# A gather that waits for the landing of the gather two ahead of it, in a graph layer on one Trainium2 core

## The chip, the cores and the metric

The kernel runs on one core of a Trainium2 chip. A core has a matrix engine (TensorE, PE in the profile; its weight loads are a row of their own, PEld), a vector engine (VectorE, DVE), an engine for pointwise functions (ScalarE, ACT), GpSimd (POOL) and a queue engine (SyncE, SP). Each engine runs its own instructions in the order in which they were built and waits on semaphores for the others. Transfers run on 16 DMA engines; a transfer raises a semaphore when its data has landed. The metric is the device time in microseconds (us) of one execution.

## The reference

Every node has a row of 128 floats. The rows are normalised, each node sums the normalised rows of its neighbours, and a small network works on the mean:

```python
N, E, D, H = 12500, 200000, 128, 512      # the sizes that come in
h = jnp.maximum(_layernorm(x, axis=-1), 0.0)
msgs = h[src]                                              # 200,000 rows, in any order
agg = jax.ops.segment_sum(msgs, dst, num_segments=n)       # dst is sorted
deg = jax.ops.segment_sum(ones, dst, num_segments=n)
agg = agg / jnp.maximum(deg, 1.0)[:, None]
t = jax.nn.relu(agg @ Wg + h @ Ws + bg)
t = jnp.tanh(t @ W1 + b1)
t = jnp.tanh(t @ W2 + b2)
return x + (t @ W3 + b3)
```

The edges are sorted by `dst`, so edges that stand together end at nodes that stand together. `src` is random: row by row, `h[src]` reads from anywhere in the table.

## The kernel before

**Setup.** The rows of `x` are normalised in pieces and stored to a table `htab` in DRAM (lines 210 to 228). The source indices are turned so that column `c` of `scol` holds the 128 indices of chunk `c` (lines 180 to 202). There are 1563 chunks of 128 edges. For 80 of them ("raw" chunks) the rows of `x` itself are gathered at the very start (line 132), and normalised later on DVE; for the other 1483 the rows come out of `htab` once it is written.

**A gather.** `gather(c)` (line 290) takes a tile `rows` of 128 x 128 floats (64 KB) from a ring of `AHEAD` = 40 buffers and issues one indirect DMA on GpSimd's queue: partition p receives the table's row that `scol[p, c]` names. GpSimd itself makes the descriptors of the transfer; that is the `DMA_INDIRECT` instruction of the profile. The engine does nothing else between the 80 raw gathers and the end.

**What a gather waits for.** Two waits stand in the built program. The first comes from the tile framework: GpSimd's transfers use eight landing semaphores in turn, so the sequencer holds a gather back, with an event instruction of its own, until the transfer that used the same semaphore last has landed, which is the gather eight ahead. The second wait stands in the gather itself: PE must have read the rows that lay in its buffer before, those of the gather 40 ahead.

**The use.** `add(c)` (line 412) multiplies the rows of a chunk by a one-hot matrix `oh` that DVE has made (`onehot`, line 339): the sum by node comes out of PE. Each of these products is two matmul records in the profile, `agg<-oh,rows` or `edge<-oh,rows`. The network's layers for blocks of 512 nodes (`layers`, line 589, and the parts that it strings together) are mixed between the products of the chunks. A loop over the chunks (line 635) writes the whole order down: it calls `gather` so far ahead that 40 chunks are open (line 651), then `add(c)`, then a step of a block's layers. PE, ACT and the stores on SP keep that order (`keep_in_program_order`). From chunk `QUICK` = 1312 on, the order of the layers' steps is planned with a pace of 1.251 us a gather (line 658), and the last blocks are small, so that little is left after the last chunk.

Of the kernel before, what the change touches and what calls it, by code (L numbers as in the profile page):

```python
# [34 lines left out]
BLK = 512  # L35
PIECE = 14
GRP = 8
NRAW = 10
RAW0 = 256
STEP = 40  # L40
# [15 lines left out]
def windowed(ctx, tc, x, src, dst, Wg, Ws, bg, W1, b1, W2, b2, W3, b3, out, flag):  # L56
    nc = tc.nc
# [12 lines left out]
    NCOL = NROW * CPR  # L70
    RAW1 = RAW0 + NRAW * STEP
    per = N * P // E
    assert D == P and H % P == 0 and per * E == N * P and RAW0 % GRP == STEP % GRP == 0
    assert all(c % GRP == 0 for c, _ in WINDOWS) and RAW1 <= WINDOWS[1][0]


    def raw(c):
        return RAW0 <= c < RAW1 and (c - RAW0) % STEP < GRP

# [3 lines left out]
    def first(w, span=per):  # L83
        return (span - w) // 2

    def window(c):
        if raw(c):
            return per * (c - c % GRP) + first(W_RAW, per * GRP), W_RAW
        w = [w for c0, w in WINDOWS if c0 <= c][-1]
# [20 lines left out]

    rsrc = const.tile([P, NRAW, GRP], I32, name="rsrc")
    rdst = const.tile([P, NRAW, GRP], I32, name="rdst")
    for t, a in ((rsrc, src), (rdst, dst)):
        a = a[RAW0 * P : RAW1 * P].rearrange("(u e) -> u e", u=NRAW)[:, : GRP * P]

        for u0, u1 in ((0, 1), (1, NRAW)):
            nc.sync.dma_start(t[:, u0:u1], a[u0:u1].rearrange("u (p k) -> p u k", p=P))
# [10 lines left out]
    raw_rows = []  # L128
    for g in range(NRAW):
        t = raws.tile([P, GRP, D], F32, name=f"raw{g}")  # L130
# [139 lines left out]

    ed = ctx.enter_context(tc.tile_pool(name="ed", bufs=3))
    ml = ctx.enter_context(tc.tile_pool(name="ml", bufs=2))
    rows_t, ohs, acc = {}, {}, {}

    class pe:

# [12 lines left out]

    def gather(c):  # L290
        r = rows_in.tile([P, D], F32, name="rows")
        nc.gpsimd.indirect_dma_start(  # L292
            out=r, out_offset=None, in_=htab,
            in_offset=bass.IndirectOffsetOnAxis(ap=scol[:, c : c + 1], axis=0),
        )
        rows_t[c] = r


# [336 lines left out]
    for c in range(NCH):  # L635
# [15 lines left out]
        while nxt < len(order) and nxt < behind + AHEAD:  # L651
            gather(order[nxt])
            nxt += 1
# [367 lines left out]
@with_exitstack  # L1021
def gnn_kernel(ctx: ExitStack, tc: tile.TileContext, *args):
    nc = tc.nc
    keep = ctx.enter_context(tc.tile_pool(name="flags", bufs=1))
    flag = keep.tile([1, 1], I32, name="flag")
    with ExitStack() as inner:
        windowed(inner, tc, *args, flag)
    outside = nc.values_load(flag, min_val=0, max_val=P)
    with tc.If(outside > 0):
        with ExitStack() as inner:  # L1030
            general(inner, tc, *args)
# [31 lines left out]
```

## Time and profile before

| | |
|---|---|
| median of 3 runs | 2302.71 us (2298.98 to 2318.72) |
| the profiled execution's own time | 2288.5 us |
| its span, first to last instruction | 2286.0 us |
| first and last gather out of `htab` start at | 119.9 us and 2237.4 us |
| first and last product of gathered rows start at | 123.6 us and 2271.9 us |
| mean granted clock of PE | 0.784 |
| data moved by GpSimd's queue | 102.53 MB in 50016 packets, 17.2% of 16 engines' time |

The page gives busy time by engine, a picture of the span in 40 slices, the DMA queues, the chain of work that ended last, and groups of like instructions. For a stretch of time, the trace lists each instruction with its start, its length and, in brackets, how long the engine stood idle before it and what ended that. "issue" there is time in which the engine waited for nothing that the profile shows, and "remote" a release whose source it can't name. Waits of a sequencer (the front of an engine, which reads instructions and waits on their semaphores) have records too, marked with a q (POOLq).

### The profile page before, as it was taken

What the parts mean: (1) busy time and instruction counts of PE and PEld (TensorE: products, weight loads), DVE (VectorE), ACT (ScalarE), POOL (GpSimd) and SP (SyncE); (2) the same over time, 40 slices, a digit from 0 to 9 for tenths busy, and PEclk for the clock granted to TensorE, in tenths of its full rate; (3) what the DMA queues carried; (4) which work ended last, traced back from release to release, by engine and by line L of the source; (5) the groups of instructions that cost most, each with busy time, mean ns of one, the idle gap of its engine ahead of it and who ended that gap; (6) DMA issues with size and microseconds to landing.
All of it is one profiled execution on the core that took longest, in us unless ns stands there. A gap on an engine that the chain in (4) does not pass through costs nothing.

```text
span 2286.0 us, 15134 instructions
## 1 busy us (share of the span) xinstructions
PE 1300.2 (57%) x4838; PEld 817.6 (36%) x4838; DVE 865.2 (38%) x1534; ACT 216.3 (9%) x352; POOL 1547.1 (68%) x1571
## 2 busy tenths in 40 slices
PE   0052263664687657666436655657646467576747
PEld 0031241342454434344224332334323234243536
DVE  5851390252353524244133331333523233233422
ACT  1100000000110101011001000101100001011112
POOL 7666676676676667677766666766676676766760
PEclk9999675786787879777777767778777778687879
DMA  6622111212221222122122121221221212122210
GB/s 171 189 80 54 46 50 47 56 46 61 57 60 48 59 59 60 46 61 58 52 57 60 45 59 48 60 60 47 58 66 42 61 48 74 48 62 56 57 51 16
DMA packets 120031, 139.03 MB, mean 61 GB/s; under 512 B 30742, under 2 KB 94098, under 8 KB 119748
## 3 DMA queue, kind: packets, MB, share of 16 engines
q0 software_dynamic: 50016, 102.53, 17.2%
q1 hardware_dynamic: 66766, 32.13, 5.2%
q10 hardware_dynamic: 3160, 3.31, 0.5%
q8 instruction: 40, 0.66, 0.1%
q14 instruction: 49, 0.40, 0.1%
HBM read 125.05 MB, written 12.82 MB: 60 GB/s over the span
## 4 chain that ended last, share of the span: by engine, by line
PE 44%; issue 26%; another core or an unknown queue 15%; DVE 5%; POOL 5%; DMA 2%; ACT 1%; SPq 0%; POOLq 0%; DVEq 0%; ACTq 0%
PE pm L279 25%; PE agg L279 14%; POOL rows L292 5%; PE edge L279 5%; DMA rows<-htab,scol 2%; ACT h L303 1%; PE pt L282 1%; DVE oh L347 1%; DVE h L176 1%; DVE agg L162 1%; DVE xt L163 1%; DMA xt<-in_x_dram 1%; DVE agg L169 1%; DVE fours L367 0%
## 5 line engine op out<-in xcount | busy, mean ns | idle before, releaser
L292 POOL DMA_INDIRECT rows<-htab,scol x1483 | 1469.0, 991 | 664.9 <-issue 300.1
L279 PE MATMUL pm<-h,w 128*128 128x512 f32 (+4 forms) x1344 | 708.0, 617 | 346.8 <-issue 189.5
L279 PE MATMUL agg<-oh,rows 128*128 128x144 f32 (+3 forms) x2122 | 447.4, 328 | 322.2 <-issue 241.5
L347 DVE TENSOR_TENSOR oh<-shared,dloc 128x1152 f32<-128x1152 f32 (+2 forms) x186 | 244.4, 1318 | 937.6 <-remote 392.2
L279 PEld LDWEIGHTS agg<-oh,rows 128*128 128x128 f32 x2122 | 387.4, 223 | 574.3 <-issue 470.3
L279 PEld LDWEIGHTS pm<-h,w 128*128 128x128 f32 x1344 | 234.2, 210 | 424.0 <-issue 251.4
L279 PE MATMUL edge<-oh,rows 128*128 128x144 f32 (+2 forms) x844 | 172.4, 316 | 87.3 <-issue 79.6
L279 PEld LDWEIGHTS edge<-oh,rows 128*128 128x128 f32 x844 | 149.2, 213 | 198.6 <-issue 179.0
L367 DVE TENSOR_TENSOR fours<-oh 128x704 bf16<-128x704 f32 x185 | 163.5, 884 | 2.3
L303 ACT ACTIVATE h<-pm,b2c 128x512 f32<-128x512 f32 (+4 forms) x112 | 70.8, 632 | 884.4 <-remote 429.1
L303 ACT ACTIVATE h<-pm,b1c 128x512 f32<-128x512 f32 (+4 forms) x112 | 69.2, 632 | 326.7 <-remote 163.1
L132 POOL DMA_INDIRECT raw<-in_x_dram,rsrc x80 | 77.2, 965 | 25.7 <-issue 24.1
L399 DVE RECIPROCAL rd<-rd 128x512 f32<-128x512 f32 (+4 forms) x28 | 81.8, 2920 | 0.0
L367 DVE TENSOR_TENSOR twos<-fours 128x384 bf16<-128x384 bf16 (+1 forms) x195 | 66.8, 343 | 2.4
L397 DVE TENSOR_SCALAR rd<-pm 128x512 f32<-128x512 f32 (+4 forms) x28 | 17.4, 621 | 127.1 <-remote 91.6
L461 DVE TENSOR_TENSOR mT<-agg,sums 128x136 f32<-128x136 f32 (+6 forms) x57 | 15.4, 271 | 120.7 <-remote 54.6
L194 PE MATMUL pm<-ident,idx_f 98*128 98x98 f32 x32 | 6.2, 377 | 89.1 <-DVE idx_f L190 56.0
L579 DVE TENSOR_TENSOR o<-pt,xb 128x512 f32<-128x512 f32 x23 | 15.8, 689 | 106.1 <-remote 50.9
L380 DVE TENSOR_TENSOR deg<-deg,cnt 128x200 bf16<-128x200 bf16 (+5 forms) x279 | 54.3, 221 | 2.6
L279 PE MATMUL agg<-ohr,raw 128*128 128x160 f32 x112 | 32.5, 387 | 35.0 <-issue 35.0
L367 DVE TENSOR_TENSOR cnt<-twos 128x200 bf16<-128x200 bf16 (+1 forms) x195 | 48.2, 247 | 3.2
L306 ACT COPY hT<-pt 128x512 f32<-128x512 f32 (+1 forms) x25 | 14.4, 577 | 350.2 <-remote 170.0
(75 smaller groups left out, 509.5 us busy)
## 6 DMA issues: line engine op xcount, KB each, us to landing
rows<-htab,scol POOLq DMA_INDIRECT x1483
hb<-htab SPq DMA_DIRECT2D x24, 256.0 KB
xb<-in_x_dram SPq DMA_DIRECT2D x23, 256.0 KB
out_dram<-o SPq DMA_DIRECT2D x23, 256.0 KB
htab<-h SPq DMA_DIRECT2D x6, 896.0 KB
xt<-in_x_dram SPq DMA_DIRECT2D x5, 896.0 KB
raw<-in_x_dram,rsrc POOLq DMA_INDIRECT x80
w<-in_L_gnn_W_dram ACTq DMA_DIRECT2D x1, 1024.0 KB
```

What stands on the lines that cost most here:

```text
L132: nc.gpsimd.indirect_dma_start(out=t[:, j, :], out_offset=None, in_=x, in_offset=bass.IndirectOffsetOnAxis(ap=rsrc[:, g, j : j + 1], axis=0),)
L162: nc.vector.tensor_reduce(stats[:, 0], xt, AX.X, ALU.add)
L163: nc.vector.scalar_tensor_tensor(xt, spread(stats[:, 0], k), -1.0 / D, xt, op0=ALU.mult, op1=ALU.add)
L169: nc.vector.tensor_reduce(stats[:, 1], sq, AX.X, ALU.add)
L176: nc.vector.scalar_tensor_tensor(h, xt, 0.0, spread(stats[:, 1], k), op0=ALU.max, op1=ALU.mult)
L279: tc.keep_in_program_order(nc.tensor.matmul(*a, **k))
L292: nc.gpsimd.indirect_dma_start(out=r, out_offset=None, in_=htab, in_offset=bass.IndirectOffsetOnAxis(ap=scol[:, c : c + 1], axis=0),)
L303: tc.keep_in_program_order(nc.scalar.activation(*a, **k))
L347: nc.vector.tensor_tensor(oh[:, :k, :w], lane[:, None, :w].to_broadcast([P, k, w]), dloc[:, g * GRP : g * GRP + k][:, :, None].to_broadcas ...
L367: nc.vector.tensor_tensor(out[:, :half, :full], ins[:, :half, :full], shifted(ins, half, half, lead, full), op=ALU.add)
L380: nc.vector.tensor_tensor(d, d, cnt[:, a0 - lo : a1 - lo], op=ALU.add)
L399: nc.vector.reciprocal(rd[:, :m], rd[:, :m])
```

## The change

Each gather but the first two is given a dependence on the landing of the gather that stands two ahead of it. `landing` is a list of the gathers' names in the order of issue.

```diff
+BEHIND = 2
...
-    rows_t, ohs, acc = {}, {}, {}
+    rows_t, ohs, acc, landing = {}, {}, {}, []
...
     def gather(c):
         r = rows_in.tile([P, D], F32, name="rows")
-        nc.gpsimd.indirect_dma_start(
+        dma = nc.gpsimd.indirect_dma_start(
             out=r, out_offset=None, in_=htab,
             in_offset=bass.IndirectOffsetOnAxis(ap=scol[:, c : c + 1], axis=0),
         )
+        if len(landing) >= BEHIND:
+            tc.add_manual_dep(
+                dma.ins, landing[-BEHIND], mybir.DependencyInfo(mybir.DependencyClass.Sync, mybir.DependencyReason.DATA),
+                reason="a gather begins when the one two before it has landed",
+            )
+        landing.append(dma.ins.name)
         rows_t[c] = r
```

In the built program a gather still has one event instruction and its own wait on PE. The event instruction now names the semaphore of the gather two ahead; that the gather eight ahead has landed follows from it. The ring of 40 buffers, the eight semaphores, the order on every engine and the data are the same, and GpSimd's program has two event instructions more.

## The prediction

> **What bounds the kernel now.** I start with the page's busy times:
>
> ```profile
> PE 1300.2 (57%) x4838; PEld 817.6 (36%) x4838; DVE 865.2 (38%) x1534; ACT 216.3 (9%) x352; POOL 1547.1 (68%) x1571
> ```
>
> No engine is full. POOL is the busiest, and nearly all of that is gathers, so I ask next what a gather waits for (the trace's answer on line 292):
>
> ```profile
> L292 POOL DMA_INDIRECT rows<-htab,scol x1483: 938/944/2728, 119.9 to 2237.4; - x186
> L292 POOLq EVENT_SEMAPHORE  x1450: 17/17/21711, 97.3 to 2235.2; - x182
> its engine sat idle before it (us, times) until:
>   issue: 300.1, 962
>   remote: 115.3, 76
>   PE agg L279: 102.4, 152
>   DMA rows<-htab,scol: 46.9, 154
>   PE pm L279: 43.7, 77
>   PE edge L279: 35.5, 54
> ```
>
> The reader is to see that 962 of the gathers start after 300.1 us of plain "issue", 0.31 us each, and that the landing of another gather (the DMA row) cost 46.9 us in 154 cases, also 0.30 each: no gather lost anything to the landing eight ahead. What did cost time is PE, through the ring of buffers. Unhindered, a gather comes every 0.944 + 0.30 = 1.245 us (the rows below). From 119.9 to 2237.4 the 1482 steps took 1.429 us each, so 272 us went to long gathers and to waits for PE. In the trace the time from a gather's start to the first use of its rows has a median of 38.7 us; only 84 of the 1483 rows are used within 3.4 us. So now **PE paces the ring** at 1.43 us a chunk, and gathers are some 30 chunks early. The limit that stands next is GpSimd at 1.245 us.
>
> **The change part by part.** It removes the wait for eight back, which costs nothing. It adds a wait that makes a loop: gather n-2 starts, lands, the sequencer sees it, gather n starts. Two such loops run side by side, so the new pace is half of one loop, or 1.245 us, or PE's 1.43 us, whichever is longest. The loop has two terms.
>
> *Start to landing.* A stretch in which PE waits for rows shows it from above:
>
> ```profile
> 172.10 0.94 POOL L292 DMA_INDIRECT rows<-htab,scol  x1 [0.30 <-DMA rows<-htab,scol]
> 173.35 0.95 POOL L292 DMA_INDIRECT rows<-htab,scol  x1 [0.30 <-issue]
> ...
> 174.75 0.82 PE L279 MATMUL agg<-oh,rows 128*128 128x144 f32 x2 [0.53 <-DMA rows<-htab,scol]
> ...
> 175.83 0.61 PE L279 MATMUL agg<-oh,rows 128*128 128x144 f32 x1 [0.27 <-DMA rows<-htab,scol]
> ```
>
> The gather of 172.10 is used at 174.75 and that of 173.35 at 175.83: 2.65 and 2.48 us. Over all rows that PE waited for, the least is 2.47, the usual 2.5 to 2.65, and about one in eight is near 3.2. From below, the gather before a gap in the queue, with the bytes moved (40 slices of the stretch from 812 to 822 us, 0.25 us each, in GB/s):
>
> ```profile
> 812.69 0.94 POOL L292 DMA_INDIRECT rows<-htab,scol  x1 [0.30 <-issue]
> 818.33 1.00 POOL L292 DMA_INDIRECT rows<-htab,scol  x1 [4.70 <-PE pm L279]
> ```
>
> ```profile
> GB/s 82 0 0 0 229 33 0 0 0 213 49 0 0 0 0 0 0 0 0 0 0 0 0 0 0 0 0 0 0 0 0 0 213 33 16 0 0 229 33 0
> ```
>
> The bytes of the gather at 812.69 move in the tenth and eleventh slice, 814.25 to 814.75, so 1.6 to 2.06 us after its start, long after its 0.94 us on POOL. Landing lies between 2.06 and 2.47 us for a plain one; the trace's semaphore records put it at 2.3 to 2.4, and with the slow ones at 2.45 on average. I take 2.45. The Trainium skill, DMA: Bandwidth & Descriptors (section on the anatomy of a SWDGE DMA), fits 2.0 us plus bytes over 436,000 per us, an estimate of 2.15 us for 64 KB; the rows are longer, and are used.
>
> *Landing to start.* Today the event wait of a gather is passed a median of 7.4 us before the gather starts, so whatever the sequencer needs after a landing is hidden behind six queued gathers. With two back, that cover is gone. Before's trace has no gather that starts straight after a landing it needed, so I bound it. From below by 0.30 us, the step between gathers whose waits are long over. From above by the first gather: the longest event wait, 21.711 us, begins at 97.3, so it ends at 119.0, and the gather starts at 119.9, 0.9 us later, with two more short waits of its own in between. Nearest is the sequencer's own pace: after the stall at 818 its records follow each other at 0.51 us for one event and one gather, and the released gather started 0.21 us after the next one's record. 0.51 + 0.21 = 0.72, plus 0.04 us that the records show between a semaphore's last step and the end of a wait: 0.76. I take that.
>
> *Sum.* 2.45 + 0.76 = 3.21 us for two gathers, 1.605 each. The two loops also push each other (a gather can't start under 1.245 us after its neighbour): stepped through with each gather's own length and landing out of this trace, the pace comes to 1.635. That is above 1.245 and above PE's 1.43, so **the landing loop sets the pace**, and the 272 us of waits for PE don't come on top: PE's slow stretches of 20 to 30 us take 12 to 18 of 40 buffers. What is behind the waiting gather on POOL is only further gathers. DVE's one-hots, ACT and SP's stores hang on PE and get more time, not less. The two added event instructions cost 17 ns each, nothing here.
>
> *The end.* The last product of gathered rows stands at
>
> ```profile
> 2271.90 0.30 PE L279 MATMUL agg<-oh,rows 128*128 128x20 f32 x2
> ```
>
> and the span ends at 2286.0, 14.1 us later; that work stays. In before the last gather (2237.4) lay 34.5 us ahead of its use because PE was behind; with PE waiting it is 2.5. So: 119.9 + 1482 x 1.635 + 2.5 + 14.1 = 2559.6, and 2.5 us outside the span (2288.5 - 2286.0): **2562 us**. This is 273.5 us over the profiled execution, which lies 14 us (0.6%) under the median of the runs; a pace set by landings doesn't carry that difference, and I add nothing for it.
>
> **The rivals.**
>
> *A: the wait is covered, no slower.* If the sequencer has the next gather ready while it waits, landing to start is 0.30 and the loop 2.75 us, 1.375 a gather. PE's 1.43 decides again, and the time is 2290 to 2300. The point at which it turns is a loop of 2.86 us, a landing to start of 0.41. For it: the step of 0.30 between gathers. Against: the 0.9 of the first gather and the pace of 0.51. The Trainium skill, same page and section, gives some 50 ns to the sequencer's dispatch; by it the loop would be about 2.5 us, and this case would hold. The recorded 0.51 us speaks against that figure.
>
> *B: PE can't keep up beside it.* If PE idles between chunks and its clock falls, its own 1.43 grows past 1.635. At half clock throughout, PE's 1300.2 busy us become 1300.2 x 0.784 / 0.5 = 2039; the 739 us more, spread over 1483 chunks, would put PE at 1.93 and the end at 119.9 + 1482 x 1.93 + 17 + 2.5, about 3000. Partly so, 2700 to 2850. For it: the granted clock does go to 0.59 in a stretch such as 797 to 817 us. Against: between 1087 and 1114, where PE waits for rows again and again, the clock is 1.00, as the row of that stretch shows:
>
> ```profile
> 1087.00:1114.00 27.00, 20.07 (x73) 10.08 (x71) 6.63 (x12) 2.06 (x3) 20.38 (x22) 1.00 0.20 51
> ```
>
> The Trainium skill, TensorE: Matmul & The Clock Gate (Part 1), says that an idle window of about 3.4 us halves PE's clock; the gaps here would be under 1.6 us, so by that rule too B is unlikely.
>
> *C: faster.* Fewer gathers in flight could land sooner and disturb DVE less (gathers longer than 0.944 us cost 69 us in all). With PE as the pace that would be worth at most some 30 us, about 2260, and needs A's cover first.
>
> **How the numbers follow.** Forecast 0.82, A 0.08, B 0.08, C 0.02. For the range: with 0.51 us from landing to start the pace is about 1.51 and the time 2377; with 0.94 (0.9 and the 0.04) it is 1.73 and the time 2700. The lower bound of 0.30 is A, left out with C, as is most of B: 2380 to 2700. A measurement of this kernel can tell about 1% from no change. Slower by over 1%: 0.82 + 0.08 = 0.90; within 1%: A, 0.08; faster: C, 0.02.
>
> **What would show it.** Gathers in the profile after should stand 1.6 us apart on average, in pairs of about 3.2; the idle time before them should be named after the landing of `rows`, some 1000 us of it, and hardly after PE. PE should use nearly every row under 4 us after the gather's start, and its waits should be for the DMA of `rows`. The event waits of POOLq should be long, not 17 ns. The last gather should start near 2540. The forecast is wrong if gathers still come at 1.25 us between waits for PE (A), if rows lie 30 us unused while the time has grown (B), or if a landing takes another time when only two are open than with eight.

## The result and the profile after

| | before | after |
|---|---|---|
| median of 4 runs each | 2301.63 us (2298.98 to 2318.72) | 2678.07 us (2673.27 to 2687.54) |
| profiled execution, and its span | 2288.5 us, 2286.0 us | 2673.27 us, 2671.0 us |
| first and last gather out of `htab` start at | 119.9 us, 2237.4 us | 113.8 us, 2653.3 us |
| mean granted clock of PE | 0.784 | 0.823 |

The changed kernel is slower: 1.1603 times the time before, 95% interval 1.1556 to 1.165. The forecast was 2562 us, +11.3%, in a range of 2380 to 2700. The direction and the mechanism came as forecast; the forecast is 116 us too small.

First the busy times of the page after:

```profile
PE 1598.2 (60%) x4838; PEld 861.3 (32%) x4838; DVE 894.4 (33%) x1534; ACT 219.3 (8%) x352; POOL 1524.0 (57%) x1571
```

GpSimd's work has not grown (1547.1 us of busy time before, in a shorter span); it stands still for longer. Next the part of the page on the chain of work that ended last, by engine and then by line:

```profile
DMA 61%; PE 19%; issue 14%; DVE 3%; POOL 3%; POOLq 0%; another core or an unknown queue 0%; SPq 0%; ACT 0%; DVEq 0%
DMA rows<-htab,scol 60%; PE pm L280 8%; PE agg L280 7%; PE edge L280 4%; POOL rows L293 3%; DVE oh L354 1%; DVE agg L163 0%; DMA xt<-in_x_dram 0%; DVE xt L164 0%; DVE h L177 0%; DVE agg L170 0%; PE pt L283 0%; POOL raw L133 0%; POOLq L293 0%
```

Before, PE held 44% of this chain and DMA 2%. Now the transfers into `rows` alone are 60% of it. The trace's answer on the gathers' line says what each gather waited for (line 293 now, line 292 before):

```profile
L293 POOL DMA_INDIRECT rows<-htab,scol x1483: 939/946/1942, 113.8 to 2653.3; - x186
L293 POOLq EVENT_SEMAPHORE  x1455: 17/17/16477, 96.3 to 2652.6; - x182
its engine sat idle before it (us, times) until:
  PE agg L280: 362.8, 514
  DMA rows<-htab,scol: 313.4, 293
  PE edge L280: 209.5, 281
  issue: 139.0, 309
  PE pm L280: 74.9, 81
...
who waited for it (us, times):
  PEld agg L280: 1074.9, 930
  PE agg L280: 653.1, 725
```

The 1482 steps from 113.8 to 2653.3 take 1.7136 us each, where they took 1.429. The idle times add up to 1103.8 us, as the page's group of these gathers has it too. More than half of that carries PE's name, and it would be easy to read "GpSimd waits for PE" out of it. It is the other way round, as the last two lines say: PE's loads stood 1074.9 us until rows landed, its products 653.1 us. The order in time shows why the names mislead. The timeline of after from 812 us, start, length, instruction and, in brackets, the idle time before it and what ended it:

```profile
812.04 0.95 POOL L293 DMA_INDIRECT rows<-htab,scol  x1 [2.43 <-DMA rows<-htab,scol]
...
813.29 0.95 POOL L293 DMA_INDIRECT rows<-htab,scol  x1 [0.30 <-issue]
...
814.65 0.64 PE L280 MATMUL edge<-oh,rows 128*128 128x144 f32 x2 [0.41 <-DMA rows<-htab,scol]
...
815.34 0.95 POOL L293 DMA_INDIRECT rows<-htab,scol  x1 [1.10 <-PE edge L280]
...
818.03 0.48 PE L280 MATMUL edge<-oh,rows 128*128 128x144 f32 x2 [1.60 <-DMA rows<-htab,scol]
...
818.63 0.95 POOL L293 DMA_INDIRECT rows<-htab,scol  x1 [1.07 <-PE edge L280]
...
821.95 0.95 POOL L293 DMA_INDIRECT rows<-htab,scol  x1 [1.11 <-PE edge L280]
```

The gather of 812.04 lands, PE uses its rows at 814.65, 2.61 us after its start, and the gather two behind it starts at 815.34. Every second gather then follows at 818.63 and 821.95: loops of 3.30, 3.29 and 3.32 us. A landing releases PE's product at once and, some 0.7 us later, a gather; so the last thing to happen before the gather is PE's product, and the idle time is named after it, though the gather waits for the same landing as PE.

The end is as it was. The last product of gathered rows

```profile
2656.82 0.30 PE L280 MATMUL agg<-oh,rows 128*128 128x20 f32 x2
```

stands 14.2 us ahead of the end of the span (14.1 before), but now 3.5 us, not 34.5, behind the last gather's start.

### The profile page after: what moved, and what is told of

The parts are those of the page before. It is cut to its first block, busy times and chain, and to the rows that moved or that the text cites. A ratio compares the mean times of both kernels' runs of the same rounds, so it can differ in the third digit from the quotient of the medians.

```text
span 2671.0 us, 15156 instructions
## 1 busy us (share of the span) xinstructions
PE 1598.2 (60%) x4838; PEld 861.3 (32%) x4838; DVE 894.4 (33%) x1534; ACT 219.3 (8%) x352; POOL 1524.0 (57%) x1571
## 4 chain that ended last, share of the span: by engine, by line
DMA 61%; PE 19%; issue 14%; DVE 3%; POOL 3%; POOLq 0%; another core or an unknown queue 0%; SPq 0%; ACT 0%; DVEq 0%
DMA rows<-htab,scol 60%; PE pm L280 8%; PE agg L280 7%; PE edge L280 4%; POOL rows L293 3%; DVE oh L354 1%; DVE agg L163 0%; DMA xt<-in_x_dram 0%; DVE xt L164 0%; DVE h L177 0%; DVE agg L170 0%; PE pt L283 0%; POOL raw L133 0%; POOLq L293 0%
## 5 line engine op out<-in xcount | busy, mean ns | idle before, releaser
L293 POOL DMA_INDIRECT rows<-htab,scol x1483 | 1445.7, 975 | 1103.8 <-PE agg L280 362.8
L280 PE MATMUL agg<-oh,rows 128*128 128x144 f32 (+3 forms) x2122 | 673.9, 413 | 664.2 <-DMA rows<-htab,scol 653.1
L280 PEld LDWEIGHTS agg<-oh,rows 128*128 128x128 f32 x2122 | 429.1, 247 | 1167.9 <-DMA rows<-htab,scol 1074.9
L280 PE MATMUL edge<-oh,rows 128*128 128x144 f32 (+2 forms) x844 | 245.4, 380 | 289.2 <-DMA rows<-htab,scol 269.0
L280 PEld LDWEIGHTS pm<-h,w 128*128 128x128 f32 x1344 | 248.3, 226 | 19.9 <-issue 16.5
L310 ACT ACTIVATE h<-pm,bgc 128x512 f32<-128x512 f32 (+4 forms) x28 | 17.7, 633 | 210.8 <-PE pm L280 210.8
L313 ACT COPY sums<-edge 128x280 f32<-128x280 f32 (+5 forms) x27 | 10.1, 375 | 270.2 <-PE edge L280 255.7
```

Of the source, the lines that this page charges most:

```text
L280: tc.keep_in_program_order(nc.tensor.matmul(*a, **k))
L293: dma = nc.gpsimd.indirect_dma_start(out=r, out_offset=None, in_=htab, in_offset=bass.IndirectOffsetOnAxis(ap=scol[:, c : c + 1], axis=0),)
L310: tc.keep_in_program_order(nc.scalar.activation(*a, **k))
L313: tc.keep_in_program_order(nc.scalar.copy(*a))
```

## The experiments

**The theory**: a gather two behind another can't start before the other has landed and the sequencer has got from there to the next gather. Half of this loop is the pace. **Its rivals**: the wait costs something of its own whatever it waits for (a toll, or a pattern of gathers that PE likes less); PE's work is the pace, and the change only spreads it; only the time from landing to start is new.

The experiments ran on three chips, called A, B and C here, each beside the kernel before on the same chip. Chips turned out to differ, so each ratio is taken on one chip. Where a time from start to landing is given, it is from a gather's start to the last of the 16 semaphore steps of its transfer, out of the trace's semaphore records, over the gathers that have at least 15 of the 16 on record.

**Wait for the third gather ahead.** Chip A, before 2291.42 us.

```diff
-BEHIND = 2
+BEHIND = 3
```

> BEHIND = 3: a gather waits for the landing of the gather three ahead; nothing else differs from the changed kernel. Theory (loop of landing and sequencer): the loop is 2.63 us from start to landing plus 0.74 us to the next start plus some 0.06 us of pushing, 3.43 us; a third of it is 1.14 us, under GpSimd's own 1.245 us and under the 1.43 us of the kernel before, so the wait is hidden and the time is that of before, 2290 to 2320 us. Rival (a toll on each gather: a wait on a recent landing keeps the sequencer from running ahead, and each gather pays its 0.28 us at any small depth): 2600 us or more. Rival (the time goes smoothly with the number of open gathers, as with a bandwidth): between the two, about 2430 us.

Measured: 2302.31 us, ratio 1.0045 (1.0019 to 1.0071). The waits of its gathers:

```profile
L293 POOL DMA_INDIRECT rows<-htab,scol x1483: 938/944/2458, 120.0 to 2253.4; - x186
...
  DMA rows<-htab,scol: 181.7, 571
```

181.7 us in 571 times is 0.32 us each, the ordinary step between gathers. A loop of some 3.4 us over three gathers is 1.14 each, under GpSimd's own 1.245, so the wait is over before it is reached. The added dependence costs at most the 0.45% measured here; the rival of a toll, which asked for 2600 us, has fallen, and so has that of a time that goes smoothly with the number of open gathers (2430 us).

**Wait for the gather just ahead.** Chip A.

```diff
-BEHIND = 2
+BEHIND = 1
```

> BEHIND = 1: a gather waits for the landing of the gather just ahead, so one is open at a time. Theory: the pace is one whole loop, 2.63 + 0.74 = 3.37 us, without pushing between two loops; 114 + 1482 x 3.37 + 20 = 5130 us, 4950 to 5250 us with landings of 2.5 to 2.7 us. Rival (two open gathers slow each other's landing): landings fall to 2.3 us or less when one is alone and the time is 4640 us or less. Rival (toll of 0.28 us on each gather): about 2700 us, as the changed kernel.

Measured: 4947.55 us, one run. The timeline of its GpSimd:

```profile
811.34 0.94 POOL L293 DMA_INDIRECT rows<-htab,scol  x1 [2.22 <-DMA rows<-htab,scol]
814.64 0.94 POOL L293 DMA_INDIRECT rows<-htab,scol  x1 [2.36 <-DMA rows<-htab,scol]
817.83 0.94 POOL L293 DMA_INDIRECT rows<-htab,scol  x1 [2.24 <-DMA rows<-htab,scol]
```

Now the whole loop stands between neighbours: 3.30 and 3.19 us here, 3.242 on average. It is 2.492 us from start to landing on average (median 2.468) and 0.750 from landing to start (median 0.737). The loop itself is as the theory has it; the time lies 2.5 us under the range given (4950 to 5250), because the landing is shorter than the 2.63 us that was put in. The rival of two open gathers slowing each other has fallen too: it asked for landings of 2.3 us or less. PE's granted clock fell to 0.567 in this run, and PE still didn't set the pace.

**The wait in the gather itself.** Chip A. The rows of eight gathers lie in one tile and there are six such tiles; PE's release of a tile then has to be waited for by one gather in eight. The wait for the landing two ahead stands in the gather itself in the others, and the event instruction ahead of it is gone (192 of them in place of 1455).

```diff
-    rows_in = ctx.enter_context(tc.tile_pool(name="rows_in", bufs=AHEAD))
+    rows_in = ctx.enter_context(tc.tile_pool(name="rows_in", bufs=AHEAD // GRP + 1))
...
-        r = rows_in.tile([P, D], F32, name="rows")
+        if len(landing) % GRP == 0:
+            eight[0] = rows_in.tile([P, GRP, D], F32, name="rows")
+        r = eight[0][:, len(landing) % GRP]
```

> The changed kernel with BEHIND = 2, but the rows of eight gathers lie in one tile (six tiles of eight for 40 single ones), so that only one gather in eight waits for PE; the other seven have the landing wait as their only one and it stands in the gather itself, with no event instruction of the sequencer ahead of it. Theory: the 0.74 us from landing to start is the event instruction and the decoding of the gather behind it, and falls to the 0.26 us that a gather showed in the kernel before between PE's release and its start; the loop is 2.63 + 0.28 = 2.91 us for seven and 3.4 us for the eighth, about 3.03 us with pushing, 1.515 us a gather: 2380 us, 2320 to 2450 us. Rival (0.74 us is the way of a landing to GpSimd, whatever carries the wait): 2678 us, no change.

Measured: 2368.51 us, ratio 1.0318 (1.0279 to 1.0358). The timeline of its GpSimd, where the names now are the true ones:

```profile
812.13 0.94 POOL L295 DMA_INDIRECT rows<-htab,scol  x1 [0.33 <-DMA rows<-htab,scol]
813.54 0.94 POOL L295 DMA_INDIRECT rows<-htab,scol  x1 [0.46 <-DMA rows<-htab,scol]
815.41 0.94 POOL L295 DMA_INDIRECT rows<-htab,scol  x1 [0.93 <-DMA rows<-htab,scol]
```

From landing to start it is 0.260 us at the median, where it was 0.738 with the event instruction (and 0.738 for the one gather in eight that still has one). On average it is 0.46 us, since the slow one in eight also holds up gathers behind it. The landing itself takes what it took, 2.56 us on average. The loop is 3.008 us and the pace 1.504. So 0.48 of the 0.74 us is the way through an event instruction to the gather behind it, and nearly four fifths of the loss go with it (3.2% is left, of 14.7% for the changed kernel on chip B below).

**The same tiles, without the wait two back**, as a control. Chip B, before 2297.72 us.

> The kernel before with the rows of eight gathers in one tile (six tiles of eight for 40 single ones) and no wait on two back: the control for the run with the wait in the gather. One gather in eight waits for PE; each waits for eight back, seven of eight within the gather. Theory: PE paces the ring, so 2290 to 2320 us as before; the run with the wait in the gather (2368 us) then owes its 3% to the landing loop. Rival (the tiles of eight cost something themselves, since a tile is free only when all eight are used): 2340 us or more. Rival (the event instructions on GpSimd's sequencer cost something in the kernel before): under 2250 us.

Measured: 2298.58 us, ratio 1.0014 (0.9986 to 1.0043). The tiles of eight cost and bring nothing in the kernel before, so what the experiment above shows is put down to the loop.

**The changed kernel with less work for PE.** Chips A and B. Of the second layer's 448 products 336 are left out, so the output is no longer the reference's.

```diff
-            for kk in range(HM):
-                yield mm, hop if m == 0 and kk == HM - 1 else 0
-                pe.matmul(
-                    p2[:, :n], w2[:, kk, m * P : (m + 1) * P], h1[:, kk, :n], start=(kk == 0), stop=(kk == HM - 1)
-                )
+            yield mm, hop if m == 0 else 0
+            pe.matmul(p2[:, :n], w2[:, m, m * P : (m + 1) * P], h1[:, m, :n], start=True, stop=True)
```

> The changed kernel with the second layer cut: each block of the 512 x 512 product takes one of its four partial products (112 of 448 products are left, so the output is not the reference's). Theory: landings set the pace, PE waits for rows anyway; the time stays at 2650 to 2690 us and PE's busy time falls by some 150 to 250 us. Rival (PE holds the kernel back at this pace, by its clock or its work): with a quarter of its products gone the time falls by 100 us or more, below 2580 us.

Measured on chip A, one run: 2633.65 us, 44 us under the 2678.07 of the changed kernel. But the landing on that chip took 2.476 us at the median against 2.547 in the trace of the changed kernel, and a shorter landing gives the same sign as PE's work. So both were run on one chip, B.

> The changed kernel once more, beside the next run on one chip, to tell what part of the 45 us by which the kernel with the cut second layer was shorter belongs to the chip. Theory (landings set the pace): the median landing is that of the next run, and with the 2.47 us that the first experiments' chip showed in place of 2.55 the time is 2620 to 2650 us there; with 2.55 us it is 2670 to 2690 us. Rival (PE's work counts at this pace): 2670 to 2690 us whatever the landing is, 40 us or more over the next run.

> The changed kernel with a quarter of the second layer's products (the output is not the reference's), beside the run before it. Theory (landings set the pace): within 15 us of the changed kernel on the same chip. Rival (PE's work counts): 40 to 50 us shorter than it.

Measured: the changed kernel 2631.03 us, ratio 1.1472 (1.141 to 1.1534); with less work for PE 2631.64 us, ratio 1.146 (1.1401 to 1.1518). The busy times of the two, changed kernel first:

```profile
PE 1576.2 (60%) x4838; PEld 854.2 (33%) x4838; DVE 894.6 (34%) x1534; ACT 219.5 (8%) x352; POOL 1523.0 (58%) x1571
```

```profile
PE 1495.7 (57%) x4166; PEld 861.7 (33%) x4166; DVE 895.8 (34%) x1534; ACT 219.7 (8%) x352; POOL 1527.3 (58%) x1571
```

672 matmul records (two for each product) and 80 us of PE's time less, and the same time: PE's work doesn't count in the changed kernel. PE's busy time fell by less than its records, since the granted clock fell too, from 0.827 to 0.689. Both have a landing of 2.474 us on this chip. That is 0.073 us shorter than in the first comparison, and over 1482 / 2 loops it is 54 us, which is more than the 44 us that could have been put down to PE on chip A.

**The kernel before with less work for PE.** Chip B, the same edit in the kernel before. The prediction called PE the pace there.

> The kernel before with a quarter of the second layer's products (336 of 448 products are left out, so the output is not the reference's). Theory (PE paces the ring there): the time falls clearly, by the 672 matmul records of 4838 that are gone, some 14% of 2117 us, to about 2000 us; GpSimd's own 1.245 us stops it at 120 + 1482 x 1.245 + 20 = 1985 us. Rival (gathers are paced by something else that PE's work does not touch, as transfers or GpSimd): 2250 us or more.

Measured: 2272.48 us, ratio 0.9897 (0.983 to 0.9963), pace 1.426 us a gather.

```profile
PE 1127.5 (50%) x4166; PEld 764.5 (34%) x4166; DVE 847.2 (37%) x1534; ACT 215.9 (9%) x352; POOL 1550.7 (68%) x1571
```

PE lost a tenth of its busy time (1247.9 us in the profile of the control with eight to a tile, on the same chip, at a clock of 0.763; here 0.704), and the time moved by 1%, not to the 2000 us that PE's work as the pace would have given. The reading "PE's work paces the ring at 1.43 us" has fallen.

**Only every other gather waits two back.** Chip C, where the kernel before takes 2041.22 us (2037.78 to 2044.04), not 2300. One loop is left and can't be pushed by a second.

```diff
-        if len(landing) >= BEHIND:
+        if len(landing) >= BEHIND and len(landing) % 2 == 1:
```

> As the changed kernel, but only every other gather waits for the landing of the one two ahead; those between wait for eight back as before. The loop is then one chain and not two that push each other. Theory (landing plus 0.74 us, and pushing for the rest): the pace is half of one plain loop, (2.56 to 2.63 + 0.74) / 2 = 1.65 to 1.685 us by the chip's landings, 2580 to 2630 us, about 50 us under the changed kernel on the same chip. Rival (there is no pushing; the rest is something each gather pays): the time of the changed kernel, 2630 us with median landings of 2.47 us and 2678 us with 2.55 us.

Measured: 2606.22 us, ratio 1.2766 (1.2743 to 1.2789). The loop is 3.355 us, against 3.36 of the changed kernel on chip B. From landing to start it is 0.782 us on average, against 0.817 there: the pushing is visible and worth some 0.035 us a loop, but on the way to the sum the landing took 0.026 more and gave most of it back. Since the chips differ, this settles only that pushing is small.

**Every other, and every third gather, with the wait in the gather itself.** Chip C, in tiles of eight as above, the gathers kept in the order of the program.

```diff
-        if len(landing) >= BEHIND:
+        if len(landing) >= BEHIND and len(landing) % 2 == 1:
```

> Rows of eight gathers in one tile, so that the landing wait stands in the gather itself, and only every other gather waits for two back. Theory (landing plus 0.26 us): a loop of 2.83 to 2.90 us, 1.42 to 1.45 us a gather, 2235 to 2285 us if PE keeps up. Rival (the kernel before is held at 1.43 us a chunk by something that counts chunks and not PE's work): 2290 us or more. Rival (0.74 us remains): 2600 us.

Measured: 2237.71 us, ratio 1.0967 (1.0939 to 1.0995); loop 2.848 us, of which 2.555 to the landing and 0.293 from there to the start. Three neighbours in the timeline of its GpSimd:

```profile
812.61 0.94 POOL L295 DMA_INDIRECT rows<-htab,scol  x1 [0.47 <-DMA rows<-htab,scol]
813.85 0.94 POOL L295 DMA_INDIRECT rows<-htab,scol  x1 [0.30 <-issue]
815.36 0.94 POOL L295 DMA_INDIRECT rows<-htab,scol  x1 [0.56 <-DMA rows<-htab,scol]
```

From 812.61 to 815.36 there are 2.75 us, and the free gather lies between. The pace is 1.424 us, so the theory's range holds, and the rival by which 0.74 us remains (2600 us) has fallen. With `% 3 == 0` in place of `% 2 == 1`:

> As the run before, but every third gather waits for two back: three gathers take 1.245 us and one loop of 2.83 to 2.90 us, 4.1 us or 1.36 to 1.38 us each. Theory A (the kernel before loses time only where rows come at GpSimd's full pace for long; a paced queue does not): 114 + 1482 x 1.37 + 20 = 2165 us, 2140 to 2200 us, faster than the kernel before. Theory B (1.43 us a chunk is a limit of its own, whatever sets the gathers): 2270 to 2310 us.

Measured: 2200.08 us, ratio 1.0776 (1.0757 to 1.0795), pace 1.399 us. The time is at the upper end of theory A's range, and the pace over its 1.36 to 1.38: the waiting loop is 2.92 us on average. It is under 1.43 all the same, so 1.43 us is no floor of this kernel on every chip. On chip C the kernel before was far under it already, so these two could be no faster than it, and theory A's "faster than the kernel before" didn't come.

**The kernel before with a thin network.** Chip C: 5 of the 26 products of a block's layers are left.

> The kernel before with the network cut to five products a block in place of 26 (one part of the first layer, one of the second and of the third are left; the output is not the reference's), so that 1176 of 4838 matmul records and over half of PE's time are gone, while the products of the gathered rows stay. Theory A (the pace of the kernel before has to do with PE's work): GpSimd's own pace, 1980 to 2050 us. Theory B (1.43 us a chunk is a limit of its own): 2230 to 2290 us again.

Measured: 2060.92 us against 2041.22, ratio 1.0098 (1.0075 to 1.0121). Its busy times and the waits of its gathers:

```profile
PE 1308.8 (64%) x3662; PEld 807.5 (39%) x3662; DVE 848.4 (41%) x1534; ACT 113.3 (6%) x184; POOL 1564.7 (76%) x1571
```

```profile
L292 POOL DMA_INDIRECT rows<-htab,scol x1483: 940/944/2615, 104.7 to 2042.0; - x186
...
  DMA rows<-htab,scol: 210.3, 690
```

Again 0.30 us a time, the ordinary step, and no gather stands idle for more than 0.31 us before it. The pace is 1.307 us: here GpSimd alone sets the time, and a quarter of PE's products less doesn't make it shorter. Why it is 1% longer is not shown. The run is no choice between its two theories, which were written for a kernel before of 2300 us; nor did PE's busy time become small, for its granted clock is 0.637 here and 0.889 to 0.896 in the kernel before on this chip. None of these kernels beats the kernel before on its chip.

## Why the prediction was right, and where it was short

*The landing loop sets the pace.* Right. One gather back gives 3.242 us a gather, two give 1.681 to 1.714, three hide the loop (1.440), and a shorter way from landing to start gives 1.504. PE's work changes nothing in the changed kernel.

*Start to landing, 2.45 us.* This is the term that was mis-sized. In the trace after it is 2.547 us at the median and 2.62 on average. (2.62 - 2.45) / 2 x 1482 is 126 us, a little more than the whole shortfall. The figure was taken between two readings, and the wrong one was given weight. In the trace of before only some 3 of the 16 semaphore steps of a landing are recorded, so the last one that is seen (2.29 us at the median, 2.42 on average) comes too early; in the trace after there are 15.4 of 16. The right row was the other: the first use of rows in a stretch where PE waits, 2.65 and 2.48 us in the lines shown. After the change the median of all first uses is 2.62 us. The estimate of 2.15 us by the Trainium skill, DMA: Bandwidth & Descriptors (section on the anatomy of a SWDGE DMA), is shorter than any landing in the runs with one or two open (the least with all 16 steps recorded is 2.36 us). Part of the shortfall is the landing of this comparison: with the 2.474 us at the median of chip B the changed kernel takes 2631 us there, 69 over the forecast. The range held the measured time with some luck. Its upper bound, 2700, comes from 0.94 us between landing and start, the term that was right; for the landing, the term that was off, it had no bound at all.

*Landing to start, 0.76 us.* Right, by 0.02: 0.738 at the median. It is 0.04 us to the end of the event's wait, as forecast, and 0.70 from there to the gather's start (0.72 forecast). On average, with the pushing of the two loops, it is 0.812; forecast were 0.76 and 0.06 a loop for the pushing.

*The ends.* The first gather starts at 113.8 us, not 119.9, and from the last gather's start to the end of the span it is 17.7 us, not 16.6. With these, 113.8 + 1482 x 1.7136 + 17.7 + 2.2 outside the span is 2673.3, the time of the profiled execution.

*PE paces the kernel before at 1.43 us.* Wrong as it was meant, though no number of the sum hangs on it. With 14% fewer matmul records the kernel before became 1% faster, with 24% fewer, on chip C, not faster at all. The waits did carry PE's name, and PE is late in them; its amount of work isn't why. What makes it late is likely the slow stretches of the last section, but this isn't shown: in every run on such a chip that is free of them, the landing loop sets the pace. The limit of 1.245 us that the prediction put next is nearly reached on chip C: 1.307 us a step with the thin network, long gathers included, and some 1.29 in the kernel before, an estimate from its time less the two ends, (2041 - 105 - 20) / 1482.

*Rival A, no slower.* Its condition, 0.30 us from landing to start, didn't come: it was 0.74. Nor would its time have followed. With the wait in the gather itself the condition held (0.260), and the kernel was still 3.2% slower, because the landing is longer than the 2.45 that A was worked out with (2.56 on average), and because the one gather in eight with an event instruction and the pushing bring landing to start to 0.46 on average. The 50 ns that the same section of the Trainium skill gives to the sequencer's dispatch are not what decides here: it takes 0.26 us with no instruction between, and 0.70 with an event instruction.

*Rival B, PE can't keep up.* PE's clock was 0.823 on average, higher than before. In the stretch that had been shown for it, it did fall, as the window's row says (stretch, length, busy time of PE, its loads, DVE, ACT and POOL, then the clock):

```profile
1087.00:1114.00 27.00, 17.98 (x45) 8.80 (x45) 12.30 (x21) 3.14 (x5) 15.28 (x16) 0.73 0.25 66
```

From 1.00 to 0.73, yet PE is idle for 9 of the 27 us there. The clock fell although no idle time of PE in that stretch is longer than 1.7 us, about the gaps that the prediction had counted on to keep it up. The rival fails because PE has time left, not because its clock holds. *Rival C, faster*: its cover, that is A's, didn't come, so it was not put to the test. There was also little to thin out. A gather comes every 1.25 us at the fastest and lands after some 2.5, so in the kernel before two or three are open at a time, and not the eight that the prediction compares with two.

*What would show it.* Pairs of gathers at 3.3 us, an idle total of 1103.8 us where some 1000 was forecast, rows used at a median of 2.62 us, and PE's waits for the DMA of `rows`: as said. The last gather started at 2653.3, not near 2540. Two more signs didn't come. The idle time was to be named hardly after PE, and 647 us of it are. And the event waits were to be long, but their records still have a median of 17 ns: for most of them only the end of the wait is recorded, though the engine demonstrably stood.

## What to carry to other kernels

A wait for a landing n back is free as long as start to landing plus landing to start, divided by n, stays under the pace that holds without it; here that is 3.2 to 3.4 us, so three back is free (0.45%) and two back costs 15 to 16%, where the kernel before takes some 2300 us. Where such a wait must be, let it stand in the waiting instruction itself and not in an event instruction ahead of it, which was worth 0.48 us a loop here at the median, and as much on average with every other gather waiting (0.782 against 0.293 us). Take the landing from the first use of the data where the reader waits for it, not from the last step that a trace with gaps happens to show; and call an engine the pace only after a kernel with less work for it has become faster.

## What the runs showed of the hardware that was not expected

- **The landing hardly depends on how many transfers are open**: 2.468 us at the median with one and 2.476 with two on the same chip; in the kernel before, with two or three, the lines shown give 2.48 to 2.65 by first use. What it takes with more, no run here shows. In the stretch shown of after, the bytes of the gather of 812.04 move between 813.5 and 814.25 us, that is 1.5 to 2.2 us after its start (40 slices from 812 to 822 us, in GB/s); most of the landing time lies ahead of the data. In the run with one open gather, at the median of 1200 gathers, the first bytes move 1.65 us after the gather's start, the last are through at 2.13, and the last semaphore step follows 0.34 us later.

```profile
GB/s 0 0 0 0 0 0 98 131 33 0 0 98 148 17 0 0 0 0 0 0 229 33 0 0 0 246 17 0 0 0 0 0 0 164 98 0 0 0 262 0
```

- **The landing differs between comparisons** by 0.07 us (2.547 at the median in the first, 2.476 and 2.474 on A and B), which a kernel that hangs on the landing turns into 2%. That it is the chip is likely, but the record doesn't name the chip of the first comparison.
- **The same kernel before takes 2041 us on one chip and 2291 to 2302 on the others.** Where it takes 2300, the traces have stretches, mostly of 10 to 50 us, in which PE's products follow each other singly and slowly, as here in the kernel before:

```profile
801.14 0.40 PE L279 MATMUL edge<-oh,rows 128*128 128x144 f32 x1 [2.52 <-issue]
803.93 1.01 PE L279 MATMUL pm<-h,w 128*128 128x512 f32 x1 [2.40 <-issue]
```

Counting stretches of at least eight products, each 0.6 to 4 us after the one ahead, that trace has 23 of them, 578 us in all, and the trace after has none. The same traces have only about 3 of 16 semaphore steps of a landing on record. In the traces from chip C neither is seen (the kernel before itself was only timed there), nor are the slow stretches where gathers come at 1.5 us or more, on any chip; there 14 to 16 of the steps are recorded. So the loss by the change may be far larger on chip C: the changed kernel was not run there, but a wait of every other gather alone cost 28%. Whether the slow stretches are the chip's, or come with the recording, was not tried and stays open.
